# Where the softmax denominators of one attention slot are folded and applied: at the end of the slot, or inside the first point of the next

## The chip, the cores and the metric

The kernel runs on one core of a Trainium2 chip. The metric is the device time of one launch, in microseconds, as the median of several executions. A NeuronCore has five engines that concern us, each with its own instruction queue that it works off in order: PE (TensorE: matrix products into PSUM banks; its weight loads are shown apart, as PEld), DVE (VectorE), ACT (ScalarE), POOL (GpSimd) and SP (SyncE, which here only starts DMA transfers). [...]

## The reference

Two layers on an image batch of 4 x 64 x 64 pixels with 256 channels, all in fp32. Layer 0 is full self-attention over the 4096 pixels of an image; its last line adds the scaled result to the input. Layer 1 is a depthwise 3x3 convolution (three outputs per channel), a two-layer perceptron with a gelu on top of it, and a local 3x3 attention.

```
# layer 0, per image: x is [4096, 256]
q, k, v = x @ Wq + bq, x @ Wk + bk, x @ Wv + bv        # q, k: 32 wide; v: 256 wide
attn    = softmax(q @ k.T, axis=-1)                    # [4096, 4096]
x       = gamma * (attn @ v) + x
# layer 1
perceived = depthwise_conv3x3(x) + b_perc              # 256 -> 768
hid       = gelu(perceived @ w_up1 + b_up1)            # 768 -> 512
h         = x + hid @ w_up2 + b_up2                    # 512 -> 256
out       = h + local_attention_3x3(h)
```

## The kernel before

**Slots and points.** An image is cut into 8 blocks of 512 pixels (8 rows). One block of queries is a *slot*; the four images give 32 slots (`NSLOT`), numbered through. In a slot the 4096 keys are worked off in 16 *points* of 256 keys each, numbered by `G` (0 to 7) and `half` (0, 1). Channels lie on the partitions, as two halves of 128 (`CH = 2`).

**What a point does.** `energy` (line 404) multiplies keys by queries into the PSUM tile `e`, of which there is one, and ACT takes the exponential into a weight tile `p` (line 409; three buffers). It runs two points ahead of its use. `product` multiplies the weights by the values and accumulates over all 16 points in the PSUM tiles `acc`. In the plain slots two banks are used; in 29 of the 32 slots (those for which `in_two_sums` is true: slot 1 and slots 3 to 30) four banks, because some points split the weights into a high part, a low part and a gap part (`ph`, `pl`, `pg`, and `oh`, `ol`, `og`) that the PE multiplies in a faster form. There are exactly four `acc` banks, so that the products of the next slot can't start before the sums of this slot have been read out. `add_up` adds the weights into `den`, for the softmax denominators; some of these adds are done by accumulating DMA transfers that POOL starts (`sent`).

**The end of a slot.** After point 15 `partial_sums` (lines 532 and 533) transposes the 512 columns of `den` on DVE and reduces them to partial sums, `parts`; in most slots the same is done for the sum of a local attention of an earlier slot (`lsum`). Then `finish` runs. It

- multiplies `parts` by a constant matrix `fold` on the PE, so that each partition gets whole denominators (line 551, tile `dps`, in one of the two small PSUM banks "m");
- takes the reciprocal, spreads it over 512 columns and transposes it on DVE (lines 554, 540, 543), and adds it on POOL to a tile that watches for overflow (line 197);
- scales the gap sums on ACT (line 561) and adds them to the main sums on DVE (line 567), which is the last read of the `acc` banks;
- multiplies by the reciprocals (line 569) and adds bias and residual into the image ring `xp` (line 575), both on DVE; at some slots POOL then copies or clears a border row of the ring (`rim`).

**Layer 1 runs in the gaps.** Each point of a slot also runs one or two jobs of layer 1 for an earlier slot, in the order of the list `jobs`. Their matrix products all go through the same two banks "m", handed out in turn (`job_bank`), so that a job's first matmul waits until DVE or ACT has read the result of the job two before it. At point 0 the jobs are the first part of `hidden_part` (PE products `hid_a` and `hid_bc`, line 779; ACT copies `hid_a`, line 792; DVE adds the two, line 786) and `local_values` (PE product `lv`, line 999; two DVE adds, line 1012). At point 1 they are, on DVE, the spreading of a local reciprocal (`local_denominator`) and the second part of `hidden_part` (`hid_de`, `hid_gf`, and DVE adds at line 786). The convolution (`perceive`, lines 662 and 666) is spread over the points by the list `share`; it takes the largest part of DVE's time.

**The last slot of an image.** In slots 7, 15 and 23 each point also ends with a value projection for the next image (`project_v`, PE line 339, ACT lines 355, 376 and 377, DVE lines 378 to 380), in a bank "m" too. That of point 15 stands between `partial_sums` and `finish`.

The order of everything is written out by hand: each engine runs its instructions in the order in which the Python code issues them. At a slot's end the kernel before has

```
            for _ in conv:
                pass
            if slot < NSLOT - 1:
                next(finish(slot))
```

and the next slot's point 0 then issues `energy`, its jobs and `product`, in this order.

Of the kernel before, what the change touches and what calls it, by code (L numbers as in the profile page):

```python
# [12 lines left out]
ALU = mybir.AluOpType  # L13
# [3 lines left out]
P = 128  # L17
# [3 lines left out]
CH = C // P  # L21
HP, WP = H + 2, W + 2
NB = 512
# [19 lines left out]
NSLOT = B * NBLK  # L43
# [6 lines left out]
SPLIT = 4096.0  # L50
# [10 lines left out]
def attention_then_perception_kernel(  # L61
# [19 lines left out]
    nc = tc.nc  # L81
# [17 lines left out]
    def unshifted():  # L99
# [6 lines left out]
        def tile_of(shape, tag, name, bufs=1):  # L106
            return pool.tile(shape, F32, tag=tag, name=name, bufs=bufs)

        def bank(tag, name):
            return psum.tile([P, NB], F32, tag=tag, name=name, bufs=dict(m=2, acc=2 * CH)[tag])  # L110
# [16 lines left out]
        def ring(slot):  # L127

            return 1 + slot % RING * RB
# [62 lines left out]
        def watch(values):  # L192

            n = values.free_size()
            for i in range(0, n, P):
                at = watched[:, : min(P, n - i)]
                nc.gpsimd.tensor_tensor(at, at, values[:, i : min(n, i + P)], ALU.add)
# [3 lines left out]
        def seen():  # L201

            i = next(free)
            return watched[:, i : i + 1]
# [12 lines left out]
        def in_two_sums(s):  # L217
            return 0 < s < NSLOT - 1 and s != LAG_PERC
# [174 lines left out]

        weights, highs, lows, gaps, sent = {}, {}, {}, {}, {}
        sums, accs, lsums, lrdens = {}, {}, {}, {}
        parts_, inverses, turneds = {}, {}, {}

        DIRECT = NSLOT - LAG_HID - 1

# [119 lines left out]
        def shared(s):  # L519

            a = s - LAG_ATT + 1
            return a if 0 <= a < DIRECT - 1 else None
# [15 lines left out]
        def on_all(values, turned, out):  # L538

            nc.vector.tensor_copy(  # L540
                squares(turned), values.unsqueeze(2).to_broadcast([P, NJ, SQ])
            )
            nc.vector.transpose(out, turned)

        def finish(s, parts=((0, RB),)):

            acc = accs.pop(s)
            n = NJ * (1 if shared(s) is None else 2)
            ps = bank("m", f"dps_{s}")[:, :n]
            given = parts_.pop(s).rearrange("p i j -> p (i j)")[:, :n]  # L550
            nc.tensor.matmul(ps, lhsT=fold, rhs=given, start=True, stop=True)
            inverse = tile_of([P, 2, NJ], "inverse", f"inverse_{s}")
            inverses[s] = inverse
            nc.vector.reciprocal(inverse.rearrange("p i j -> p (i j)")[:, :n], ps)

            rden = sums.pop(s)[:, 1, :]
            on_all(inverse[:, 0, :], turneds[s][:, 0, :], rden)
            watch(inverse.rearrange("p i j -> p (i j)")[:, :n])
            os = [tile_of([P, NB], "o", f"o_{s}_{c}", 2) for c in range(CH)]
            for o, gap in zip(os, acc[CH:]):  # L560
                nc.scalar.mul(o, gap, -1.0 / (SPLIT + 1.0))
            for r0, r1 in parts:
                n = slice(r0 * W, r1 * W)
                for c, o in enumerate(os):
                    total = acc[c]
                    if in_two_sums(s):
                        nc.vector.tensor_tensor(o, acc[c], o, ALU.add)
                        total = o
                    nc.vector.scalar_tensor_tensor(
                        o[:, n], total[:, n], gam_parts[:, 0:1], rden[:, n], ALU.mult, ALU.mult,  # L570
                        accum_out=seen(),
                    )
                for c, o in enumerate(os):
                    dst = xv[:, c, ring(s) + r0 : ring(s) + r1, 1 : 1 + W]
                    nc.vector.scalar_tensor_tensor(
                        dst, o[:, n].rearrange("p (h w) -> p h w", w=W), gbv[:, c : c + 1], dst,
                        ALU.add, ALU.add,
                    )
                if len(parts) > 1:
                    yield  # L580
            if s < NSLOT - 1:
                rim(s)
            yield

        def rim(s):


            g = s % NBLK
            if g == RING - 1:
                nc.gpsimd.tensor_copy(xv[:, :, 0, :], xv[:, :, RP - 2, :])  # L590
            elif g == NBLK - 1:
                nc.gpsimd.memset(xv[:, :, 0, :], 0.0)
            if g == RING:
                nc.gpsimd.tensor_copy(xv[:, :, RP - 1, :], xv[:, :, 1, :])
            elif (g == 0 and s > 0) or s == NSLOT - 2:
                nc.gpsimd.memset(xv[:, :, RP - 1, :], 0.0)
# [596 lines left out]
        for slot in range(NSLOT):  # L1193
# [52 lines left out]
            for point in range(points):  # L1246
# [23 lines left out]
                    load_forms(*soon)  # L1270
                for do in jobs[point]:
                    do()
                if slot == NSLOT - 1 and point == NHC + 2 * RING:
                    nc.sync.dma_start(out=wup1[:, :MULT, C:], in_=turned_up)
                product(slot, G, half)
# [55 lines left out]
                        fetch(slot + 1 + G + 2)  # L1331
            for _ in conv:
                pass
            if slot < NSLOT - 1:
                next(finish(slot))


# [15 lines left out]


        finishing = finish(last, ((0, 1), (1, RB)))
        next(finishing)
        run((guide, last - 2, 0, 0), (guide, last - 2, 1, 0))
# [392 lines left out]
    with tc.manual_schedule():  # L1750
        wv, gam, wperc, bperc, wup1, bup1, wup2, bup2, blqk, blv = unshifted()
# [50 lines left out]
```

## Time and profile before

| what | value |
|---|---|
| median of 3 runs | 3248.11 us (3247.27 to 3250.21) |
| the profiled execution, its own time | 3249.86 us |
| its span, first to last instruction | 3248.1 us |
| PE busy | 3218.2 us (99%) |
| DVE busy | 2866.3 us (88%) |
| ACT busy | 1449.8 us (45%) |
| POOL busy | 724.1 us (22%) |
| one full slot, from `dps` to `dps` (1028.67 to 1123.78) | 95.11 us, with PE busy 94.37 and DVE 88.41 |

The profile is one execution. Busy shares are averages over all slots. In the timeline a line gives the start in microseconds, the duration (of a group: from its first start to its last end), engine, source line, operation, tiles and count; brackets at the end hold the idle time of that engine just before, and what ended it. The ends of matmuls are modelled, so the time that the PE spends on something is best read from one start to the next.

### The profile page before, as it was taken

The page shows a single profiled execution, that of the slowest core. Times are in us where ns is not written, and L with a number is a line of the kernel's source. Part 1 is how long each engine was busy: PE and PEld are TensorE (multiplying, and loading weights), DVE is VectorE, ACT ScalarE, POOL GpSimd, SP SyncE. Part 2 cuts the span into 40 slices and gives each one's busy share as a digit, 9 for nine tenths or more (in the row PEclk, how much of TensorE's full clock was granted, in tenths as well). Part 3 has the DMA queues.
Part 4 walks back from the last instruction along what each step waited for, and adds up shares of the span by engine and source line. Part 5 has one row for each costly group of instructions (what it writes and reads, how often), then busy time and mean ns, then how long its engine had stood idle before and what let it go on. Part 6 is the DMA issues. An engine that isn't in the chain of part 4 may idle for free.

```text
span 3248.1 us, 37927 instructions
## 1 busy us (share of the span) xinstructions
PE 3218.2 (99%) x12286; PEld 2223.2 (68%) x12286; DVE 2866.3 (88%) x4380; ACT 1449.8 (45%) x1845; POOL 724.1 (22%) x970
## 2 busy tenths in 40 slices
PE   9999999999999999999999999999999999999998
PEld 5557767766776677676767767776677677667655
DVE  4779899898999999988999999998799999999895
ACT  4434444444444444444444444444444444444331
POOL 3201122221222221222122222211221122222021
PEclk9999999999999999999999999999999999999999
DMA  7767766777667777667766677776777666777100
GB/s 254 222 165 202 194 187 191 202 230 205 196 187 200 211 211 191 186 196 243 205 191 193 184 200 213 208 194 192 253 210 195 190 191 185 201 210 204 49 25 28
DMA packets 289964, 616.58 MB, mean 190 GB/s; under 512 B 97424, under 2 KB 98464, under 8 KB 289632
## 3 DMA queue, kind: packets, MB, share of 16 engines
q1 hardware_dynamic: 228608, 409.47, 40.5%
q0 software_dynamic: 53472, 191.17, 24.8%
q10 hardware_dynamic: 7680, 13.44, 1.1%
q8 instruction: 102, 1.67, 0.2%
q14 instruction: 102, 0.84, 0.1%
HBM read 386.24 MB, written 76.41 MB: 142 GB/s over the span
## 4 chain that ended last, share of the span: by engine, by line
PE 75%; DVE 17%; issue 3%; DMA 2%; ACT 1%; POOL 1%; SPq 0%; ACTq 0%; DVEq 0%; POOLq 0%
PE acc L435 19%; PE acc L458 11%; PE dx L836 5%; PE e L404 5%; DVE perc L666 5%; PE hid_bc L779 5%; PE hid_de L779 4%; PE hid_gf L779 4%; PE acc L446 4%; PE v L339 3%; PE lv L999 3%; PE g L932 3%; PE lo L1133 2%; PE hid_a L779 2%; DVE den L513 2%
## 5 line engine op out<-in xcount | busy, mean ns | idle before, releaser
L666 DVE SCALAR_TENSOR_TENSOR perc<-xp,wb,perc 128x526 f32<-128x526 f32 (+1 forms) x1356 | 941.2, 758 | 1.5 <-ACT perc L662 1.4
L435 PE MATMUL acc<-p,v 128*128 128x512 f32 x1872 | 854.5, 592 | 0.2 <-ACT v L355 0.2
L409 ACT ACTIVATE p<-e 128x1024 f32<-128x1024 f32 x512 | 524.3, 1024 | 546.6 <-PE e L404 490.5
L435 PEld LDWEIGHTS acc<-p,v 128*128 128x128 f32 x1872 | 351.7, 190 | 341.9 <-issue 328.2
L478 POOL DMA_DIRECT2D sent<-p x235 | 201.3, 857 | 1125.6 <-ACT p L409 948.9
L404 PE MATMUL e<-qa,ka 128*128 128x512 f32 x1024 | 368.3, 440 | 2.0 <-ACT p L409 1.1
L414 ACT ACTIVATE ph<-p 128x1024 fp32r<-128x1024 f32 x203 | 214.3, 1056 | 213.2 <-PE acc L458 131.6
L506 DVE SCALAR_TENSOR_TENSOR pg<-pl,ph 128x1024 fp32r<-128x1024 f32 x203 | 267.2, 1316 | 9.0 <-PE e L404 0.5
L502 DVE TENSOR_TENSOR pl<-p,ph 128x1024 fp32r<-128x1024 f32 x203 | 252.2, 1242 | 18.5 <-ACT ph L414 16.8
L458 PE MATMUL acc<-ph,v 128*128 128x512 f32 x812 | 264.0, 447 | 0.2 <-DMA v<-packed_h 0.2
L404 PEld LDWEIGHTS e<-qa,ka 128*128 128x128 f32 x1024 | 189.5, 189 | 88.2 <-issue 45.7
L420 ACT ACTIVATE oh<-p 128x512 fp32r<-128x512 f32 x150 | 94.5, 630 | 317.6 <-PE acc L446 265.4
L836 PE MATMUL dx<-hid,wup 128*128 128x512 f32 x512 | 229.8, 592 | 0.0
L458 PE MATMUL acc<-pl,vf 128*128 128x512 f32 x812 | 223.3, 397 | 0.0
L458 PE MATMUL acc<-pg,vf 128*128 128x512 f32 x812 | 218.7, 391 | 0.9 <-DVE pg L506 0.9
L504 DVE TENSOR_TENSOR den<-den,p 128x1024 f32<-128x1024 f32 x161 | 207.1, 1287 | 5.7 <-ACT p L409 5.3
L1088 POOL TENSOR_TENSOR lsum<-lsum,lp 128x99 f32<-128x99 f32 (+1 forms) x179 | 208.8, 1173 | 11.7
L458 PEld LDWEIGHTS acc<-ph,v 128*128 128x128 f32 x812 | 148.2, 189 | 51.3 <-issue 26.8
L458 PEld LDWEIGHTS acc<-pl,vf 128*128 128x128 f32 x812 | 152.7, 188 | 37.1
L458 PEld LDWEIGHTS acc<-pg,vf 128*128 128x128 f32 x812 | 152.5, 188 | 37.2 <-DVE pg L506 1.4
L802 ACT ACTIVATE hid<-hid,bup 128x512 f32<-128x512 f32 x120 | 80.2, 715 | 211.0 <-DVE hid L786 211.0
L672 DVE TENSOR_TENSOR perc<-perc 128x262 f32<-128x262 f32 x360 | 167.6, 486 | 6.3
(217 smaller groups left out, 4953.3 us busy)
## 6 DMA issues: line engine op xcount, KB each, us to landing
sent<-p POOLq DMA_DIRECT2D x287, 512.0 KB, 6.2
vf<-packed_f SPq DMA_DIRECT2D x203, 512.0 KB, 5.4
v<-packed_h SPq DMA_DIRECT2D x200, 512.0 KB, 4.4
ka<-packed SPq DMA_DIRECT2D x1016, 64.0 KB, 2.8
vo<-packed_o SPq DMA_DIRECT2D x150, 256.0 KB, 4.1
xp<-in_x SPq DMA_DIRECT2D x30, 528.0 KB, 6.1
packed_f<-vlg POOLq DMA_DIRECT2D x28, 512.0 KB, 4.5
xc<-in_x SPq DMA_DIRECT2D x56, 256.0 KB, 3.9
```

What stands on the lines that cost most here:

```text
L404: nc.tensor.matmul(e[:, i, :], lhsT=keys[s, G][:, bass.ts(2 * half + i, P)].bitcast(F32R), rhs=queries[s].bitcast(F32R), start=True, stop= ...
L409: nc.scalar.activation(p, e, AF.Exp)
L414: nc.scalar.activation(high.bitcast(F32R), weights[s, G, half], AF.Identity, scale=BELOW)
L435: nc.tensor.matmul(accs[s][c], lhsT=v[:, i, bass.ts(c, P)], rhs=p[:, i, :], start=(first and i == 0), stop=(last and i == 1),)
L458: nc.tensor.matmul(accs[s][to + c], lhsT=w[:, i, bass.ts(c, P)].bitcast(F32R), rhs=x[:, i, :].bitcast(F32R), start=(to > 0 and n == 0 and ...
L502: nc.vector.tensor_tensor(low.bitcast(F32R), p, high, ALU.subtract)
L504: nc.vector.tensor_tensor(den, before, p, ALU.add)
L506: nc.vector.scalar_tensor_tensor(gap.bitcast(F32R), low, -SPLIT, high, ALU.mult, ALU.add)
L666: nc.vector.scalar_tensor_tensor(acc, win, wt, acc, ALU.mult, ALU.add)
L779: nc.tensor.matmul(ps[:, n * C : (n + 1) * C], lhsT=w(j), rhs=rows_of(mixes[s, j][:, kind, :]), start=(j == 0), stop=(j == MULT - 1),)
L836: nc.tensor.matmul(ps, lhsT=wup2[:, d, bass.ts(c, P)], rhs=hids[s][:, d, :], start=(d == 0), stop=(d == NHC - 1),)
L1088: nc.gpsimd.tensor_tensor(to, to, near_ws[block, half][:, t_, of, :], ALU.add)
```

## The change

The read-out of the `acc` banks (lines 561 and 567) is cut out of `finish` into a function of its own, `evacuate`, which stays at the end of the slot. The rest of `finish` (fold, reciprocal, spreading, scaling, residual, rim) is issued in point 0 of the next slot, behind that point's jobs and ahead of its `product`. This is so for the 29 slots with four banks; slots 0, 2 and 31 stay as they were. No instruction is added or removed: compiled, PE's queue differs in the place of the 29 `dps` products, DVE's queue in the order of some 14 instructions at each of the 29 boundaries, and the queues of ACT, POOL and SP hold the same instructions in the same order.

```
+        def evacuate(s):
+            acc = accs.pop(s)
+            os = [tile_of([P, NB], "o", f"o_{s}_{c}", 2) for c in range(CH)]
+            for o, gap in zip(os, acc[CH:]):
+                nc.scalar.mul(o, gap, -1.0 / (SPLIT + 1.0))
+            if in_two_sums(s):
+                for c, o in enumerate(os):
+                    nc.vector.tensor_tensor(o, acc[c], o, ALU.add)
+                acc = os
+            evacuated[s] = os, acc
+
         def finish(s, parts=((0, RB),)):
 
-            acc = accs.pop(s)
             n = NJ * (1 if shared(s) is None else 2)
...
             watch(inverse.rearrange("p i j -> p (i j)")[:, :n])
-            os = [tile_of([P, NB], "o", f"o_{s}_{c}", 2) for c in range(CH)]
-            for o, gap in zip(os, acc[CH:]):
-                nc.scalar.mul(o, gap, -1.0 / (SPLIT + 1.0))
+            if s not in evacuated:
+                evacuate(s)
+            os, totals_ = evacuated.pop(s)
             for r0, r1 in parts:
                 n = slice(r0 * W, r1 * W)
-                for c, o in enumerate(os):
-                    total = acc[c]
-                    if in_two_sums(s):
-                        nc.vector.tensor_tensor(o, acc[c], o, ALU.add)
-                        total = o
+                for o, total in zip(os, totals_):
                     nc.vector.scalar_tensor_tensor(
                         o[:, n], total[:, n], gam_parts[:, 0:1], rden[:, n], ALU.mult, ALU.mult,
...
                 for do in jobs[point]:
                     do()
+                if slot and point == 0 and in_two_sums(slot - 1):
+                    next(finish(slot - 1))
...
                 product(slot, G, half)
...
             for _ in conv:
                 pass
-            if slot < NSLOT - 1:
+            if in_two_sums(slot):
+                evacuate(slot)
+            elif slot < NSLOT - 1:
                 next(finish(slot))
```

More of the change, by code (lines that the diff above doesn't have):

```diff
@@ L395, in unshifted @@
         sums, accs, lsums, lrdens = {}, {}, {}, {}
-        parts_, inverses, turneds = {}, {}, {}
+        parts_, inverses, turneds, evacuated = {}, {}, {}, {}
         DIRECT = NSLOT - LAG_HID - 1
```

## The prediction

> **What bounds the kernel now.** I read the page first (busy shares and the chain that ended last), then PE's waits, then the timelines of PE and DVE around the ends of slots.
>
> ```profile
> PE 3218.2 (99%) x12286; PEld 2223.2 (68%) x12286; DVE 2866.3 (88%) x4380; ACT 1449.8 (45%) x1845; POOL 724.1 (22%) x970
> ...
> PE 75%; DVE 17%; issue 3%; DMA 2%; ACT 1%; POOL 1%; SPq 0%; ACTq 0%; DVEq 0%; POOLq 0%
> ```
>
> PE is never idle for long, yet DVE holds 17% of the chain: somewhere PE waits for DVE. PE's waits say where (time in all, times, longest):
>
> ```profile
> PE dps L551 <- DVE parts L533: 8.6, 20, 1.0
> PE hid_a L779 <- ACT vh L377: 2.5, 3, 1.6
> PE hid_bc L779 <- ACT hid L792: 1.8, 3, 0.6
> ```
>
> All three stand at the ends of slots, and no other PE wait sums to over 1.2 us. Their 12.9 us are too small, because a matmul's modelled end hides the first part of a wait. So I take start to start. PE at the end of slot 10:
>
> ```profile
> 1024.22 3.59 PE L435 MATMUL acc<-p,v 128*128 128x512 f32 x8
> 1028.67 0.41 PE L551 MATMUL dps<-parts,fold 128*128 128x32 f32 x2 [0.85 <-DVE parts L533]
> 1028.92 0.70 PE L404 MATMUL e<-qa,ka 128*128 128x512 f32 x2
> 1029.46 1.46 PE L779 MATMUL hid_a<-perc,wup 128*128 128x256 f32 x6
> ...
> 1033.34 1.89 PE L999 MATMUL lv<-wlv,h 128*128 128x256 f32 x8
> 1035.07 3.17 PE L435 MATMUL acc<-p,v 128*128 128x512 f32 x7
> ```
>
> and at the end of slot 3, where the partial sums were ready in time:
>
> ```profile
> 326.45 3.59 PE L435 MATMUL acc<-p,v 128*128 128x512 f32 x8
> 329.88 0.29 PE L551 MATMUL dps<-parts,fold 128*128 128x16 f32 x2
> 330.02 0.70 PE L404 MATMUL e<-qa,ka 128*128 128x512 f32 x2
> ...
> 336.18 2.31 PE L435 MATMUL acc<-p,v 128*128 128x512 f32 x5
> ```
>
> From the first of the eight `acc` products to the next slot's first one it is 10.85 us in the first case and 9.73 in the second, for the same work: slot 10 loses 1.12 us, of which 0.1 is that `dps` takes 0.25 after a wait and 0.14 without one. Energy, `hid_a`, `hid_bc` and `lv` (6.15 us of PE) need nothing from `dps`; they only stand behind it.
>
> **What the Trainium skill says.** *Perfetto Trace Analysis*, "Identifying the Most-Contended Engine": matmul occupancy is no measure of headroom, since matmuls are pipelined. The trace agrees: 0.85 us of idle time is shown where 1.12 are lost. *PSUM — Partial Sum Buffer*, "Engine vs sequencer instructions": DVE's queue is strictly first in, first out, and matmuls start in program order. The trace agrees: energy, whose operands were there, waits behind `dps`. So an order is a cost, on both engines.
>
> **What the change removes from PE.** `dps` goes behind `lv`. I compared each of the 29 boundaries with its unstalled form (6.72 us from the last `acc` product to the next slot's first, as after slot 3; with the last value projection, 1.73 us, in slots 7, 15, 23; after slot 1 the form has other jobs, and only its late and slow `dps` counts):
>
> - after slot 4: 1.28; after 10, 18, 26: 1.12 each; after 11, 19, 27: 1.02 each. Sum 7.70
> - 15 boundaries at 0.44 to 0.52 (after 5, 6, 8, 9, 12 to 14, 16, 17, 20 to 22, 28 to 30). Sum 7.40
> - after 1, 24, 25: 0.38, 0.22, 0.39; after 3 nothing. Sum 0.99
> - after 7 and 15: 1.63 each; after 23: 2.70. Sum 5.96
>
> Together 22.05 us. The last group is not a wait for `parts`:
>
> ```profile
> 2336.25 0.71 PE L404 MATMUL e<-qa,ka 128*128 128x512 f32 x2
> 2338.52 1.56 PE L779 MATMUL hid_a<-perc,wup 128*128 128x256 f32 x6 [1.56 <-ACT vh L377]
> 2340.68 1.56 PE L779 MATMUL hid_bc<-perc,wup 128*128 128x256 f32 x6 [0.60 <-ACT hid L792]
> ```
>
> `hid_a` takes the bank of the last projection, read by ACT until 2338.5; `hid_bc` takes that of `dps`, read by the reciprocal (L554, 2340.29 to 2340.64). ACT's copy is only named because it ended then. With `dps` out of the turn, `hid_a` gets the bank of the projection before, long read, and `hid_bc` that of the last one: after 7 and 15 `hid_bc` would start at its own pace after it is free; after 23 `hid_bc` would be due at 2337.95 and still wait 0.57. That leaves **21.5 us**.
>
> **What it moves, and who waits then.** On PE `dps` now waits for `parts` (long done), and for its bank, which DVE's `hid_bc` add frees. `lv` takes 1.73 us; the add needs 0.27 to start (as after the later `hid_bc`: last product over at 1051.92, add at 1052.19) and 0.60 to run. 0.87 under 1.73: no wait, if DVE is free. Behind `dps` stands `product`, which needs the `acc` banks. DVE at the same boundary:
>
> ```profile
> 1027.93 0.69 DVE L533 TENSOR_REDUCE parts<-turned 128x16 f32<-128x512 f32 x1
> 1029.12 0.36 DVE L554 RECIPROCAL inverse<-dps 128x32 f32<-128x32 f32 x1 [0.50 <-PE dps L551]
> ...
> 1033.37 1.42 DVE L575 SCALAR_TENSOR_TENSOR xp<-o,gbv,xp 128x512 f32<-128x512 f32 x2
> 1034.70 0.68 DVE L786 TENSOR_TENSOR hid<-hid_bc,hid 128x512 f32<-128x512 f32 x1
> ...
> 1041.76 0.69 DVE L786 TENSOR_TENSOR hid<-hid_de,hid 128x512 f32<-128x512 f32 x1 [2.82 <-PE hid_de L779]
> ...
> 1044.35 0.69 DVE L786 TENSOR_TENSOR hid<-hid_gf,hid 128x512 f32<-128x512 f32 x1 [1.44 <-PE hid_gf L779]
> ```
>
> DVE loses time, because it now waits for PE's `hid_bc` and `lv` ahead of work that it could do at once. Worked out after slot 10, with starts from this timeline: partial sums end 1028.62; two read-outs (0.69, 0.72) to 1030.0, four us ahead of `product` (1033.95 instead of 1035.07). `hid_bc` is over at 1032.08, its add runs 1032.35 to 1032.95; `lv` is over at 1033.81, its adds (0.65) end at 1034.75. Then the reciprocal (`dps` was there at 1034.26) and its spreading (1.49) to 1036.25, scaling (1.35) to 1037.6, residual (1.33) to 1038.9, the first `den` add (1.14), a convolution step (0.67) and the local reciprocal (1.17) to 1041.9. The `hid_de` add could start at 1041.76 - 1.12 = 1040.64, so it is 1.25 late; it and its second add take 1.15, to 1043.05. `hid_gf` is ready at 1044.35 - 1.12 = 1043.23: **DVE has caught up**. The 4.26 us that it idled before `hid_de` and `hid_gf` pay for the new waits. Where PE loses 0.5 now, DVE reaches `hid_gf` with more to spare; after slot 7 just in time; after 23 some 0.2 late, which the next idle time (0.37 ahead of the later `hid_bc` add) takes up. From there to the slot's end nothing changes relative to PE; the tightest place is `pg`, ready 1.3 us before its product (at 996 and 1091).
>
> The first `den` add also frees the `p` buffer that ACT's exponential of point 3 needs. That one starts near 1040.1 (1039.17 before) and is over by 1041.2; energy needs the single `e` tile at 1046.1 (1047.18 - 1.12). Hidden by nearly 5 us. POOL's second watch add waits until some 1035.2, the border row of the ring until 1039; POOL's next start is at 1040.49, and SP's and ACT's queues keep their order. All at nothing. `hid_de` and `hid_gf` need their banks 3 us and more after DVE has read them.
>
> **The sum.** 3248.1 - 21.5 = 3226.6 of span. The profiled execution took 3249.86, 1.75 over the median of 3248.11; the saving put to the median gives **3226.6**.
>
> **Rivals.**
>
> - *Only the shown idle time goes* (10%). The waits that pipelining hides return as refills; 12.9 us are saved: 3235. Against it: slot 3's boundary runs the same work in 9.73 us.
> - *The wait moves to `pg`* (4%). From the `hid_gf` add to `parts` DVE has next to no gap (76.97 busy of 78.7 us), so it could be that DVE sets the slot's length, and PE waits at `pg` for what it gained at `dps`. Then only the 5.4 us of slots 7, 15 and 23 remain at most: 3243 to 3248. Against it: DVE restarts in each slot from `hid_gf`, which PE sets, and has 88.41 us of work in 95.11.
> - *DVE loses more than its idle time pays* (5%): slower. One mechanism: DVE's queue, held at `hid_bc` and `lv`, comes to `pl` and `pg` late. It decides from 0.18 + 0.37 + 1.3 = 1.85 us beyond my schedule. Were it out by 3.5 us, each slot would lose 1.65 and gain 0.76: 28 x 0.9 = 25 us, 3273.
> - *The change isn't what it says*: the compiled queues show all 29 `dps` moved and nothing added.
>
> **Chances.** The forecast has 81%, by itself 3223 to 3231 (a boundary class mis-sized by 0.15 us moves 4). A measurement can tell about 0.2%, 6.5 us. Faster 0.91, same 0.04, slower 0.05. The range 3223 to 3237 takes in the first rival and leaves out the rest.
>
> **What would show it.** Right: no wait at `dps`; near 6.72 us from the last `acc` product to the next slot's first at each boundary without a projection; DVE idle ahead of `hid_bc` (some 2.3 us) and `lv` (1.1), little ahead of `hid_de`; PE idle down from 29.9 us (3248.1 - 3218.2) to about 17. Wrong: a new PE wait at `pg`, at `dps` for its bank, or at the first `acc`.

## The result and the profile after

The changed kernel takes **3226.75 us** (median of 4 runs, 3226.65 to 3227.8) beside 3247.89 us of the kernel before on the same chip (4 runs, 3247.27 to 3250.21): ratio 0.9934, 95% interval 0.9917 to 0.9952. The profiled execution took 3227.80 us with a span of 3226.1, that is 22.0 us less span than before. The forecast was 3226.6.

On the page of the kernel after, the busy times, and the shares of the chain that ended last:

```profile
PE 3208.3 (99%) x12286; PEld 2224.1 (69%) x12286; DVE 2864.3 (89%) x4380; ACT 1449.7 (45%) x1845; POOL 735.9 (23%) x970
...
PE 97%; DVE 1%; DMA 1%; SPq 0%; ACT 0%; issue 0%; ACTq 0%; POOL 0%; DVEq 0%
```

PE has the same 99% as before. What tells the two kernels apart is the chain: DVE held 17% of it and now 1%. PE is idle for 17.8 us (3226.1 - 3208.3) instead of 29.9. The longest of PE's waits after (time in all, times, longest):

```profile
PE qk L269 <- DMA xc<-in_x: 1.9, 2, 1.7
PE e L404 <- DMA ka<-st: 1.3, 1, 1.3
PE e L404 <- ACT p L409: 1.1, 1, 1.1
...
PE acc L458 <- DVE pg L506: 1.0, 1, 1.0
```

`dps` is not among them any more, and nothing that recurs in each slot has come in its place; the one wait at `pg` is in slot 1, where the kernel before has it too (0.9 us). PE's timeline at the end of slot 10 (start, duration, group; `hid_a` and `hid_bc` are line 785 now, `lv` 1005, `dps` 561; a product in plain fp32 stands as two records, so that four products are x8):

```profile
1017.64 3.60 PE L435 MATMUL acc<-p,v 128*128 128x512 f32 x8
1020.67 1.02 PE L404 MATMUL e<-qa,ka 128*128 128x512 f32 x2
1021.53 1.46 PE L785 MATMUL hid_a<-perc,wup 128*128 128x256 f32 x6
...
1025.41 1.89 PE L1005 MATMUL lv<-wlv,h 128*128 128x256 f32 x8
1027.14 0.30 PE L561 MATMUL dps<-parts,fold 128*128 128x32 f32 x2
1027.28 3.25 PE L435 MATMUL acc<-p,v 128*128 128x512 f32 x7
```

From the first of the eight `acc` products to the next slot's first it is 9.64 us, where it was 10.85. Some 0.09 of these 1.21 us come back behind it: the first product after `dps` takes 0.51 us to the next start instead of 0.43. The periods below count that in. DVE at the same boundary, where the brackets show its new idle times:

```profile
1021.94 1.28 DVE L552 TENSOR_TENSOR o<-acc,o 128x512 f32<-128x512 f32 x2
1025.68 0.69 DVE L792 TENSOR_TENSOR hid<-hid_bc,hid 128x512 f32<-128x512 f32 x1 [2.47 <-PE hid_bc L785]
1027.34 0.75 DVE L1018 TENSOR_TENSOR lv<-lv,blv 128x256 f32<-128x256 f32 x2 [0.97 <-PE lv L1005]
1028.02 0.35 DVE L564 RECIPROCAL inverse<-dps 128x32 f32<-128x32 f32 x1
...
1035.19 0.65 DVE L792 TENSOR_TENSOR hid<-hid_de,hid 128x512 f32<-128x512 f32 x1
...
1036.64 0.69 DVE L792 TENSOR_TENSOR hid<-hid_gf,hid 128x512 f32<-128x512 f32 x1 [0.34 <-PE hid_gf L785]
```

DVE pays 2.47 and 0.97 us at `hid_bc` and `lv`, has no idle time left at `hid_de`, and is back in step at `hid_gf` with 0.34 us to spare. Before, it idled 2.82 and 1.44 us at the last two. The idle time has moved from behind the work to ahead of it.

Slot by slot, the period being the time from one slot's first `acc` product to the next slot's:

| slots | period before | after | gain | forecast |
|---|---|---|---|---|
| 1; 3 | 63.47; 90.99 | 63.12; 90.89 | 0.35; 0.10 | 0.38; 0 |
| ordinary full ones | 94.43 to 94.53 | 94.00 to 94.02 | 0.43 to 0.52 | 0.44 to 0.52 (25: 0.39) |
| 10, 18 | 95.22 | 94.11 | 1.12 | 1.12 |
| 11, 19, 27 | 95.12 | 94.10 | 1.02 | 1.02 |
| 4 | 92.13 | 90.89 | 1.25 | 1.28 |
| 7, 15 | 133.62 | 132.00 | 1.62 | 1.63 |
| 23 | 135.03 | 132.72 | 2.30 | 2.70 - 0.57 |
| 24; 26 | 94.55; 95.23 | 94.03; 94.51 | 0.52; 0.72 | 0.22; 1.12 |

The gains of slots 1 to 30 sum to 21.5 us. A further 1.3 us of this execution came before the end of slot 0, which the change doesn't touch. Some 0.8 were lost behind slot 30. Of these, 0.24 are a wait at a later `hid_a` of slot 31; it comes with the change, since it stands in `no_image_ends` below too (0.25) and not in `image_ends_only`, which leaves the end of slot 30 as it was.

### The profile page after: what moved, and what is told of

It reads as the page before. It is cut to its first block, busy times and chain, and to the rows that moved or that the text cites. A ratio compares the mean times of both kernels' runs of the same rounds, so it can differ in the third digit from the quotient of the medians.

```text
span 3226.1 us, 37976 instructions
## 1 busy us (share of the span) xinstructions
PE 3208.3 (99%) x12286; PEld 2224.1 (69%) x12286; DVE 2864.3 (89%) x4380; ACT 1449.7 (45%) x1845; POOL 735.9 (23%) x970
## 4 chain that ended last, share of the span: by engine, by line
PE 97%; DVE 1%; DMA 1%; SPq 0%; ACT 0%; issue 0%; ACTq 0%; POOL 0%; DVEq 0%
PE acc L435 25%; PE acc L458 17%; PE e L404 7%; PE dx L842 7%; PE acc L446 6%; PE hid_bc L785 5%; PE hid_de L785 5%; PE hid_gf L785 5%; PE lv L1005 3%; PE g L938 3%; PE v L339 3%; PE lo L1139 3%; PE s L1046 3%; PE hid_a L785 2%; DVE perc L672 1%; PE qk L269 1%
## 5 line engine op out<-in xcount | busy, mean ns | idle before, releaser
L404 PE MATMUL e<-qa,ka 128*128 128x512 f32 x1024 | 376.3, 448 | 2.4 <-DMA ka<-st 1.3
L842 PEld LDWEIGHTS dx<-hid,wup 128*128 128x128 f32 x512 | 96.7, 189 | 98.5 <-issue 93.4
```

Of the source, the lines that this page charges most:

```text
L404: nc.tensor.matmul(e[:, i, :], lhsT=keys[s, G][:, bass.ts(2 * half + i, P)].bitcast(F32R), rhs=queries[s].bitcast(F32R), start=True, stop= ...
L842: nc.tensor.matmul(ps, lhsT=wup2[:, d, bass.ts(c, P)], rhs=hids[s][:, d, :], start=(d == 0), stop=(d == NHC - 1),)
```

## The experiments

The theory: PE's queue stood behind `dps`, which waited for DVE's `parts`; DVE pays for the new order out of idle time. The rivals: only the read-out's place counts; the ends of images gain nothing of their own; DVE has no room, and what was gained goes to a later wait. An edit is shown against the changed kernel where nothing else is said. Each experiment was timed beside the kernel before; what it loses or gains slot by slot is read from one profiled execution.

**1. The read-out of `acc` ahead of the fold, both at the slot's end** (`readout_first`). DVE reads the sums out ahead of the reciprocal, as in the change; PE's order is that of before.

```
-                if slot and point == 0 and in_two_sums(slot - 1):
-                    next(finish(slot - 1))
...
             if in_two_sums(slot):
                 evacuate(slot)
-            elif slot < NSLOT - 1:
+            if slot < NSLOT - 1:
                 next(finish(slot))
```

> The early read-out of the acc banks alone: evacuate at the slot's end, and the rest of finish right behind it, also at the slot's end, so that dps stays ahead of the next slot's energy. Theory A (PE pays for work that stands behind dps in its queue): dps waits for the partial sums as before, so 25 boundaries keep their loss; the reciprocal comes 1.4 us later behind the two read-outs, which at the ends of slots 7, 15 and 23 holds the bank of hid_bc 1.4 us longer: 3 x 1.4 = 4 us lost, about 3252 us. Rival B (the acc banks read out earlier are what lets the next slot's product start earlier): most of the gain is here, 3226 to 3235.

Measured: 3248.82 us (3247.51 to 3252.32) beside 3247.58, ratio 1.0005 (0.9997 to 1.0014). As expected, the read-out's place gives nothing; the fold has to leave PE's way. But the 4 us to be lost at the ends of images did not come: from the last `acc` product to the next slot's first one it stayed 10.08 us after slots 7 and 15, although the reciprocal ran 1.2 us later behind `dps`. The timeline of this kernel at the end of slot 7, PE, then ACT and DVE:

```profile
742.25 1.56 PE L785 MATMUL hid_a<-perc,wup 128*128 128x256 f32 x6 [0.49 <-ACT vh L377]
744.41 1.56 PE L785 MATMUL hid_bc<-perc,wup 128*128 128x256 f32 x6 [0.60 <-ACT hid L798]
...
743.94 0.42 ACT L798 COPY hid<-hid_a 128x256 f32<-128x256 f32 x1
...
745.22 0.35 DVE L564 RECIPROCAL inverse<-dps 128x32 f32<-128x32 f32 x1
```

`hid_bc` starts 0.05 us after ACT's copy of `hid_a` is over (744.36) and 0.8 ahead of the reciprocal. So it does not wait for the bank of `dps`, as the prediction had it, but for ACT's copy, as the profile had said: of the two banks "m" one holds `dps` until the reciprocal has read it, so `hid_bc` has the other, that of `hid_a`. The two banks are not handed out strictly in turn, as was said above.

**2. The read-out moved along with the rest** (`all_moved`): the whole of `finish` in the next slot's point 0.

```
-            if in_two_sums(slot):
-                evacuate(slot)
-            elif slot < NSLOT - 1:
+            if slot < NSLOT - 1 and not in_two_sums(slot):
                 next(finish(slot))
```

> The whole of finish, its read-out of the acc banks included, in the next slot's point 0 behind the jobs; nothing at the slot's end. Theory A: PE no longer waits at dps, but the first acc product of the next slot waits for the read-outs, which DVE reaches only behind the hid_bc and lv adds, the reciprocal and its spreading: after slot 10 at 1036.25 + 1.41 = 1037.7 where the product is due at 1033.95, 3.7 us; 29 x 3.7 less the 21.5 gained is 86 lost, about 3334 us. If the place of the read-out does not matter: 3227.

Measured: 3229.97 us (3229.95 to 3229.99), ratio 0.9946 (0.9927 to 0.9964). The expectation was wrong by 104 us. The timeline of this kernel at the end of slot 10:

```profile
1025.16 1.09 ACT L549 ACTIVATE o<-acc 128x512 f32<-128x512 f32 x2
...
1029.14 3.68 PE L435 MATMUL acc<-p,v 128*128 128x512 f32 x8
...
1031.36 1.25 DVE L552 TENSOR_TENSOR o<-acc,o 128x512 f32<-128x512 f32 x2
```

The next slot's products start 2.2 us *before* DVE reads the sums. They wait only for ACT's scaling of the gap sums, over at 1026.25: the new slot's first two accumulators take the two gap banks, and the banks that DVE reads are not needed before the first gap product, in point 2, some 19 us later. What this document says of the four `acc` banks above (that no product can start before all sums are read out) holds for the gap sums alone. By the two profiled executions the separate `evacuate` is worth about 2 us (spans 3228.1 and 3226.1): 1.78 in slot 2 and 1.04 at a `hid_a` of slot 31 that waits for DVE, less 0.4 by which slot 26 is shorter here.

**3. The fold behind `energy`, ahead of the jobs** (`behind_energy`): about 0.9 us later than before on PE instead of 6.

```
+                if slot and point == 0 and in_two_sums(slot - 1):
+                    next(finish(slot - 1))
                 for do in jobs[point]:
                     do()
-                if slot and point == 0 and in_two_sums(slot - 1):
-                    next(finish(slot - 1))
```

> As the change, but the rest of finish stands in point 0 right behind energy and ahead of the jobs: dps moves by one energy (0.46 us) only. Theory A in amounts: the 15 boundaries where the partial sums were late by 0.35 to 0.41 lose nothing more, the seven where they were late by 0.9 to 1.2 keep 0.5 to 0.8 (4.4 us in all), and the ends of slots 7, 15 and 23 keep their 5.4 us whole, because dps still takes its bank ahead of hid_a. Gain 21.5 - 4.4 - 5.4 = 11.7: about 3236 us, and 10.1 and 11.1 us from the last acc product to the first at the ends of slots 7, 15 and of 23. Rival C (PE only saves one restart per boundary, whatever the distance): 3227. Rival D (dps must get behind the small products altogether, a partial move gives nothing): 3248.

Measured: 3237.96 us (3237.32 to 3239.44), ratio 0.9971 (0.996 to 0.9982). Ordinary boundaries come to 6.73 to 6.81 us, so the whole wait of about half a microsecond is covered. The late ones (after 4, 10, 11, 19, 26) stay at 7.13 to 7.37, and the ends of images at 10.08, 10.08 and 11.13, as before. Cover is worth what it lasts: one matmul group hides 0.5 us, not 1.1. The boundaries after 17, 18 and 27 were 7.12, 7.70 and 8.05 in this execution. They fit too: in `readout_first`, with `dps` in its old place, the same three stood at 7.57, 8.16 and 8.53 (7.18, 7.84 and 7.74 in the kernel before), since in both kernels DVE idles 0.46 us instead of 0.10 at one place of each of these slots; why it does is open. They too are 0.45 to 0.48 shorter here. With the boundary after slot 1 (6.23 us instead of 5.16: `dps` waited 1.18 us for its `parts`) they account for the 2 us that are missing to the 3236 expected.

**4 and 5. The change at the ends of images alone, and everywhere else alone.**

```
+        def moved(s):
+            return in_two_sums(s) and s % NBLK == NBLK - 1     # 5: s % NBLK < NBLK - 1
...
-                if slot and point == 0 and in_two_sums(slot - 1):
+                if slot and point == 0 and moved(slot - 1):
...
-            if in_two_sums(slot):
+            if moved(slot):
```

> The change at the ends of slots 7, 15 and 23 alone; the other 26 boundaries as before. Theory A (two causes: late partial sums, and at these three ends the turn of the two small PSUM banks): 1.62 + 1.62 + 2.3 = 5.5 us, about 3242.4. If these ends gained nothing of their own, and the 5.5 us of their slots came from elsewhere: 3248.

> The change at the 26 boundaries other than the ends of slots 7, 15 and 23. Theory A (the two causes add up): 21.5 - 5.5 = 16.0 us, about 3232. If DVE's lag from one slot to the next couples them, the two halves would not add to 21.5.

Measured: `image_ends_only` 3242.80 us (3241.55 to 3246.19), ratio 0.9985 (0.9979 to 0.9992); its periods of slots 7, 15 and 23 gain 1.70, 1.70 and 2.39. `no_image_ends` 3232.11 us (3231.2 to 3232.44), ratio 0.9951 (0.9938 to 0.9965). By medians of the runs beside them 4.8 and 15.7 us: together 20.5 of the 21.1 of the whole. Over slots 1 to 30 of the profiled executions it is 5.6 and 16.7, a little more than the 21.5 of the whole; each takes in 0.35 us that the kernel before had lost in slot 23, and in its one execution only. The parts are independent, and each has its forecast size (5.4 and 16.1) as well as these figures can tell.

**6 and 7. How much more DVE work fits in** (`dve_plus2`, `dve_plus5`): from the changed kernel, with 2 or 5 more operations of 0.72 us each on DVE behind the residual. They take the maximum of a finished sum with itself, which changes nothing.

```
-            rden = sums.pop(s)[:, 1, :]
+            den_s = sums.pop(s)
+            rden = den_s[:, 1, :]
...
+            if in_two_sums(s):
+                for _ in range(2):                                # 7: range(5)
+                    nc.vector.tensor_tensor(den_s[:, 0, :], den_s[:, 0, :], den_s[:, 0, :], ALU.max)
```

> The changed kernel with 2 idle DVE operations (maximum of a 128x512 tile with itself, about 0.69 us each) behind the residual of each of the 29 slots: 1.4 us more for DVE per boundary, 40 us in all. Theory A (PE sets the pace, DVE has room): DVE's idle time before hid_gf and the later hid_bc is 0.34 + 0.37 us, and pg is ready 1.29 us early in six slots and 2.17 in the others: room for 2.0 us and 2.9 us, so nothing is lost, 3227 to 3228. Rival E (DVE sets the pace): each added microsecond shows, 3227 + 40 = 3267.

> The same with 5 idle DVE operations, 3.45 us per boundary, 100 us in all. Theory A: beyond the room, 1.45 us in the six slots with 1.29 at pg and 0.57 in the 17 with 2.17: 8.7 + 9.7 = 18 us, about 3245, with PE waiting at pg. Rival E: 3227 + 100 = 3327. If DVE has more room than worked out: 3227.

Measured: two operations 3230.24 us (3229.41 to 3231.41), ratio 0.9947 (0.9933 to 0.996), some 2 us over the 3227 to 3228 expected. The full slots' periods moved by 0.05 us at most, save for 0.6 and 0.2 in slots 24 and 25, where PE waited for a transfer of `v` (the kernel before has such a wait in slot 24, the changed one in slot 26). What the dose itself cost is 1.1 us in slot 2, and 1.45 in slot 31, where a `hid_a` of PE waits for DVE: there it found no room at all.

Five operations 3266.32 us (3265.38 to 3267.7), ratio 1.0058 (1.0043 to 1.0074): the kernel is now slower than before. 105 us of work cost 39.6, where 18 were expected. In PE's waits of this kernel `e` has come to the top, and `pg` is there once only, in slot 1:

```profile
PE e L404 <- ACT p L409: 11.0, 26, 2.9
...
PE acc L458 <- DVE pl L502: 3.1, 6, 0.5
...
PE acc L458 <- DVE pg L506: 0.6, 1, 0.6
```

The timeline some 29 to 34 us into slot 10 shows the wait at `e`: DVE, ACT, PE.

```profile
970.07 0.69 DVE L796 TENSOR_TENSOR hid<-hid_gf,hid 128x512 f32<-128x512 f32 x1
970.80 1.34 ACT L812 ACTIVATE hid<-hid,bup 128x512 f32<-128x512 f32 x2 [6.76 <-DVE hid L796]
973.97 1.03 ACT L409 ACTIVATE p<-e 128x1024 f32<-128x1024 f32 x1
975.05 0.73 PE L404 MATMUL e<-qa,ka 128*128 128x512 f32 x2 [0.29 <-ACT p L409]
```

DVE's late add into `hid` holds ACT's gelu, ACT's next exponential stands behind the gelu in ACT's queue, and PE's energy waits for the `e` tile that this exponential reads. From start to start this costs 0.52 to 0.56 us in each ordinary or tight slot (the tight ones are 10, 11, 18, 19, 26 and 27). But it is only half of the loss, and not what sets it. The table of waits hides the rest, in the way that the prediction warned of. In slot 12, 56 us in, DVE and PE:

```profile
1188.93 1.22 DVE L506 SCALAR_TENSOR_TENSOR pg<-pl,ph 128x1024 fp32r<-128x1024 f32 x1
1190.21 1.20 PE L458 MATMUL acc<-pg,vf 128*128 128x512 f32 x4
```

PE's first gap product starts 0.06 us after DVE's `pg` is over (1190.15), and no idle time is shown, since the end of the product ahead of it is modelled later than that. From start to start the products that read `pg` lose another 0.38 to 0.44 us in each ordinary slot. DVE itself is not held up by PE's wait at `e`: from its `hid_bc` add 17 us into the slot to this `pg` it stays 2.94 us behind its times in the changed kernel. By this reckoning the slot would have lost as much at `pg` without the path through ACT; experiment 8 bears it out.

Together it is 0.95 to 1.07 us in each ordinary slot (0.57 expected) and 1.84 to 1.87 in the tight ones, where `pl` is late as well (1.45 expected; 1.44 in slot 26, which had lost 0.4 in the changed kernel's execution). Slots 7, 15 and 23 lose nothing. All these slots thus lose some 28 us, where 18 were expected; the rest is 3.27 in slot 2 and some 6 in slot 31, which the expectation did not count. The room was 3.62 - 0.97 = 2.6 us in an ordinary slot and 1.8 in a tight one (3.62 us is what the five operations took).

**8. The fold behind the product, one place further back** (`behind_product`).

```
-                if slot and point == 0 and in_two_sums(slot - 1):
-                    next(finish(slot - 1))
...
                 product(slot, G, half)
+                if slot and point == 0 and in_two_sums(slot - 1):
+                    next(finish(slot - 1))
```

> As the change, but the rest of finish stands behind point 0's product instead of ahead of it. PE does the same work without a wait; DVE, which stands at the reciprocal, waits for dps 3.4 us longer, of which it loses 2.95. Theory A: the room of 2.0 us is passed by 0.95 in six slots (5.7 us) and that of 2.9 by next to nothing: about 3233 us. If DVE's order at this place costs nothing: 3227.

Measured: 3247.45 us (3245.12 to 3249.34), ratio 0.9997 (0.9989 to 1.0006). The direction was right, but not some 6 us go, the whole gain does. DVE's line of the reciprocal in this kernel:

```profile
1036.17 0.36 DVE L564 RECIPROCAL inverse<-dps 128x32 f32<-128x32 f32 x1 [2.82 <-PE dps L561]
```

DVE now idles a third time, for 2.82 us, and the room from experiment 7 is used up in the ordinary slots too. Slot 12 again, DVE and PE, first in this kernel, then in the changed one:

```profile
1182.75 1.22 DVE L506 SCALAR_TENSOR_TENSOR pg<-pl,ph 128x1024 fp32r<-128x1024 f32 x1
1182.97 1.10 PE L458 MATMUL acc<-pl,vf 128*128 128x512 f32 x4
1184.03 1.20 PE L458 MATMUL acc<-pg,vf 128*128 128x512 f32 x4
```

```profile
1174.10 1.22 DVE L506 SCALAR_TENSOR_TENSOR pg<-pl,ph 128x1024 fp32r<-128x1024 f32 x1
1176.58 1.10 PE L458 MATMUL acc<-pl,vf 128*128 128x512 f32 x4
1177.52 1.09 PE L458 MATMUL acc<-pg,vf 128*128 128x512 f32 x4
```

In the changed kernel `pg` is over 2.2 us before PE reads it; here PE starts 0.06 us after its end (1183.97), again without idle time shown. From start to start the ordinary slots lose 0.2 to 0.4 us, nearly all of it at `pg`, and the six tight ones 1.07 to 1.10 at `pl` and `pg` (slot 26, less its 0.4: 0.73). DVE's chain is later by 2.9 us, so the room was again 2.6 and 1.8 us. At `e` neither kind of slot loses anything: the path through ACT gives way later than `pg` does. Slot 2 loses 3.2, where energy waits for an exponential whose `p` buffer a `den` add of DVE frees too late:

```profile
186.97 0.73 PE L404 MATMUL e<-qa,ka 128*128 128x512 f32 x2 [2.71 <-ACT p L409]
...
185.90 1.02 ACT L409 ACTIVATE p<-e 128x1024 f32<-128x1024 f32 x1 [10.47 <-DVE den L504]
```

Slot 31 loses 4.5 at `hid_a` and `hid_bc`. In all, the tight slots make 6 us of the loss, the ordinary ones 5, and slots 2 and 31, which the expectation left out, 8; the spans are 3244.3 and 3226.1. The place of `dps` itself costs PE nothing more: from the first `lv` product to the first of `hid_de` it takes 5.84 us here and 5.85 in the changed kernel.

**9 and 10. The operand ready early instead of the fold late** (`no_local_parts` from the kernel before, `no_local_parts_after` from the changed one): `partial_sums` without its second transposition and reduction.

```
+                if i:
+                    nc.vector.tensor_copy(parts_[s][:, 1, :], parts_[s][:, 0, :])
+                    continue
```

> The kernel before, in its old order, but its partial sums are ready earlier: the second transposition and reduction of partial_sums (of the local attention's sum, 0.71 + 0.69 us on DVE in slots 4 to 30) are left out and replaced by a 128x16 copy of the first ones, so that the local attention is scaled by wrong denominators. Theory A (PE pays for waiting, the place of dps costs nothing if its operand is there): the partial sums are late by 0.11 to 1.16 us and come 1.3 earlier, so the wait goes at every boundary but that of slot 1: 7.70 + 7.40 + 0.61 = 15.7 us, about 3232 us, with the ends of slots 7, 15 and 23 as before. Rival F (dps ahead of energy costs PE by its place): 3247.

> The same 1.3 us per slot of DVE work left out of the changed kernel, 35 us in all. Theory A (after the change PE sets the pace, DVE only has to arrive in time): nothing is gained, 3226 to 3227.5. If DVE still sets part of the pace: below 3222.

Measured: 3232.61 us (3231.99 to 3234.31), ratio 0.9953 (0.994 to 0.9967), so 15.8 us saved with `dps` in its old place, where 15.7 were expected; and 3229.00 us (3227.22 to 3230.1), ratio 0.9939 (0.9925 to 0.9952), from the changed kernel. PE's first waits in the former:

```profile
PE hid_a L782 <- ACT vh L377: 2.5, 3, 1.6
PE hid_bc L782 <- ACT hid L795: 1.8, 3, 0.6
```

The wait at `dps` is gone and those of the image ends are untouched. So the place of `dps` costs nothing by itself; what costs is that the operand is late there. And after the change, less work on DVE buys nothing: PE sets the pace. The tenth kernel even lies 1 us of span above the changed one (3227.2 and 3226.1), but that stands ahead of slot 1, whose first `acc` product comes at 115.67 us instead of 113.85 (115.19 in the kernel before); slots 1 to 30 take 2870.8 and 2871.2 us.

## Why the prediction was right

- **The bound** (PE's order, not its busy share): right. Experiments 1 and 9 exclude the read-out and the place of `dps`; 3 shows the wait shrinking by about as much as is put ahead of it.
- **Start to start instead of shown idle time**: right, and it carries the size. 21.5 us were summed, 21.5 came in slots 1 to 30; the shown waits were 12.9, and PE's idle time on the page fell by 12.1. The Trainium skill (*Perfetto Trace Analysis*, "Identifying the Most-Contended Engine") says that busy matmuls are no measure of headroom; here 99% stood on both pages. That the medians agree to 0.2 us is in part luck: the 1.3 us before slot 1 and the 0.8 behind slot 30 are in no term of the sum.
- **The ends of images**: the amount was right for slots 7 and 15 (1.62 for 1.63). For slot 23 it was 1.95 for 2.13: its boundary keeps 0.74 us over those of 7 and 15, where 0.57 were forecast. (The 2.30 of the table take in the 0.35 that the execution of the kernel before had lost elsewhere in slot 23.) One of the two reasons was wrong. The step "`hid_bc` takes that of `dps`, read by the reciprocal" fails by experiment 1: it took the bank of `hid_a` and waited for ACT's copy. It comes out alike because `hid_a` no longer waits for the projection, so its copy is early. I had put a named releaser aside for a bank order that I had only inferred.
- **DVE catches up**: right. The Trainium skill (*PSUM — Partial Sum Buffer*, "Engine vs sequencer instructions") has DVE's queue strictly in order, and the timeline agrees: the reciprocal stands behind the adds of `hid_bc` and `lv`. The schedule gave 0.18 us to spare at `hid_gf` after slot 10; 0.34 was measured. What was wrong is that the slots would differ in this. The spare time is 0.31 to 0.35 in all full slots, also after slot 23, where 0.2 too late was forecast, since DVE waits 0.96 or 0.97 us for PE's `lv` at every boundary, so that `lv` now times its chain.
- **"Behind `dps` stands `product`, which needs the `acc` banks"**: wrong for the banks that DVE reads (experiment 2). It did no harm, because the read-out stays early in the change.
- **The point from which DVE decides** (1.85 us beyond the schedule, at `pl` and `pg`): right in place, and in size for the six tight slots (1.8); in ordinary slots it is 2.6. Beyond it a path through ACT's gelu and exponential gives way too: no loss there with DVE 2.9 us late (experiment 8), 0.5 with 3.6 (experiment 7). The prediction followed DVE to its direct readers on PE only, which did no harm here. What it took for all slots alike is not so: slot 2 has some 0.4 us of room, slot 31 none, which fits the 0.24 us that the change itself loses there.
- **Small terms**: slots 24 and 26 were off by +0.3 and -0.4, and cancel. Both are waits for a transfer of `v` within one execution: the kernel before was held up so in slot 24, and stood the less at that slot's end; the changed one in slot 26.

## What to carry to other kernels

A short product whose operand comes late costs all that stands behind it in PE's queue: move it behind work that is ready, and size the gain from start to start against a boundary that does the same work without the wait, not from the idle time shown. Read experiments in the same way: two of these lost time at `pg` in every ordinary slot, and their lists of waits did not show it. Then count what the other engine now waits for, follow it through every engine down to the next point that the first one sets, and test the room with a dose of added work: here one place too early left half of the gain, and one place too late lost it all, 8 us of it in slots 2 and 31, which none of the sums had looked at. Where the profile names a releaser that fits, test it before putting a bank order of one's own in its place.

## What the hardware showed that was not expected

- A `dps` group that does not wait takes PE 0.14 us to the next start, and the product behind it then 0.08 us more than usual: 0.51 instead of 0.43 for a 128x512 product, 0.31 instead of 0.23 for an energy. The sum of 0.22 is the same in both places. After a wait it is 0.25 to the next start.
- A read-out of PSUM by DVE can be 2.2 us behind the start of the next sums and cost nothing in 27 of 29 slots, as only the banks taken first have to be free.
- 105 us of added DVE work cost 39.6 us, and a dose of two fifths of it only 3.5: room shows only beyond its edge.
- PE can wait for DVE without any idle time in its profile: at `pg` 0.2 to 0.4 us a slot were lost where PE started 0.06 us after DVE was done and its brackets were empty.
